# A spectral token mixer and FP8 MLP: one layout of quarter tiles for the whole spectrum

## The chip, the cores and the metric

The kernel runs on one core of a Trainium2 chip. The metric is the device time of one execution in microseconds (us), the median of several runs. One launch computes the whole layer, all weights and tables included, from HBM to HBM in float32 with the quantised MLP in between.

## The reference

The input x is (8, 128, 128, 96): batch, height, width, channel. The layer is

```python
x = x + conv(layernorm_c(x))          # a global filter in the Fourier domain
t = x as tokens
x = t + ffn(layernorm_t(t))           # an MLP in float8 with float16 accumulation

# conv
x_pre = soa1_scale * relu(x @ w1.T)**2 + soa1_bias        # 96 -> 192 channels
xf    = rfft2(x_pre, over h and w)                         # 128 x 65 complex, 192 channels
filt  = cubic resize of three small complex filters to 128 x 65
r     = softmax over the 3 filters of an MLP of mean(x) and mean(relu(bn(x @ sp_w.T)))
xsp   = irfft2(xf * sum_s r[s] * filt[s])
y     = xsp @ w2.T                                         # 192 -> 96 channels

# ffn, q8 = rounding to float8e5, q16 = rounding to float16
h = relu(q16(q16(q8(x) @ q8(W1).T) + q8(b1)))              # 96 -> 384
y = q16(q16(q8(h) @ q8(W2).T) + q8(b2))
```

## The kernel before

Each of the 8 batches passes through three streams.

*Stream a* (`before`) works by units of four image columns w, 32 units a batch. x is read twice: as `xb` in blocks of 16 columns with h on the partitions, for the layer norm's statistics (`measure`, and on GpSimd, ACT and DVE the reciprocal root r), and as `xT`, half-blocks of 8 columns with the channel on the partitions. r goes through HBM (`store_r`, L650) and comes back copied to 96 partitions (`load_r`, L654). `scale` (L659, DVE) multiplies four columns of xT by r into one of three `zT` tiles; both inputs are read with a step of 8 elements, since w is the innermost index of xT and rB. `project` (L672, TensorE) multiplies by w1 and sp_w, ACT applies relu and the square, `transform` (L701) takes the real Fourier transform along h, and the result goes to HBM as Y, one row of (w, 192 channels) for each of the 128 row frequencies.

*Stream s* (`spectrum`) works by groups g of four such rows, 31 full ones and two special ones (frequencies 32 and 96, 0 and 64), 33 a batch. `load_y` (L842) brings four rows with w on the partitions, in runs of 768 bytes. `along_w` (L874) is a matmul along w with the channel on the output partitions. 192 channels are more than 128 partitions, so for the two rows of a pair the first 128 channels make a full tile each, and the remaining 64 of both share a third; `pack` (L866, GpSimd) copies those side by side into `yb`. `filters_of` (L887) makes the filters with 64-column tiles, DVE (L913, L916) multiplies, GpSimd (L923, L938, L940) adds and turns back to a real basis, giving `xf`. For every two groups (16 pairs a batch), the channels are mixed with w2 into two PSUM banks `pv`, one for each row of the pair: `mix_low` first clears the banks with matmuls of zeros (L971) and adds the shared tile in quarters of the 128x128 array (64 rows by 64 columns, L984); `mix` (L995) adds the two full tiles. Two copies on ACT (L1006, L1018) and a matmul (L1011) follow, and V goes to HBM.

*Stream c* (`after`) works by units of four columns in blocks of 16. `load_v` (L1117, L1118) reads x into `xr` and V into `vin`; `last` (L1123) finishes the inverse transform, `residual` (L1131) adds xr into `t`, then layer norm, rounding to float8, and the MLP: `first` (L1170), `accumulated` (L1177, ACT, to float16), `biased` (L1181, DVE: bias and maximum with 0 for each of three tiles of 128 hidden channels), `hidden` (L1185, ACT, to float8), `second` (L1192), then L1203, L1207, L1210 and the store (L1213).

The streams of different batches overlap: a of one batch runs beside s of the batch before and c of the one before that. The order of the instructions on each engine is fixed when the kernel is built. Every step is entered by `at(time, ...)` with a due time (the stream's start plus the unit's number times its period plus an offset from the table `O` or `OWN`) and the steps it comes after; `in_order` takes the steps by due time as their predecessors and PSUM banks allow, and the engines then follow that order. Loads and small stores are issued from SyncE, the stores of Y and V from ACT.

Of the kernel before, what the change touches and what calls it, by code (L numbers as in the profile page):

```python
# [56 lines left out]
NG = 31  # L57
# [210 lines left out]
def _columns(p, r):  # L268

    if p < NP - 1:  # L270
        return [(g, cs) for g in (2 * p, 2 * p + 1) for cs in range(2)]
    return [(NG - 1, 0), (NG - 1, 1)] + [(NG, 0), (NG, 1)] * (r == 0) + [(NG + 1, 0)]
# [98 lines left out]
def metaformer_kernel(ctx: ExitStack, tc: tile.TileContext, a: dict, out: bass.AP):  # L371
    nc = tc.nc
    x, xT = a["x"], a["xT"]
# [49 lines left out]
    zeros = const.tile([128, 64], mybir.dt.bfloat16, name="zeros")  # L423

    NZT = 3
    zTs = [const.tile([C + 1, QW, 128], F32, name=f"zT{i}") for i in range(NZT)]
# [8 lines left out]
    w2A = load(T_CONST, "w2A", [128, C], a["w2T"][:128, :])  # L435
    w2B = const.tile([128, C], F32, name="w2B")
# [4 lines left out]
    b1q = const.tile([128, NHC], F32, name="b1q")  # L441
# [3 lines left out]
    def projection(sp):  # L445
# [36 lines left out]
        def others():  # L482
            for i in range(2):
                nc.sync.dma_start(out=w2B[64 * i : 64 * i + 64, :], in_=a["w2T"][128:, :])
            make_identity(nc, ident)
            nc.vector.tensor_copy(ident8, ident, saturate=False)
            nc.vector.memset(ones, 1.0 / (H * W))
            nc.vector.memset(zeros, 0.0)

            nc.vector.tensor_scalar(soa_bias, soa_bias, 128.0, None, ALU.mult)  # L490
# [6 lines left out]
    def filters(sp):  # L497
# [38 lines left out]
        def weights():  # L536
# [15 lines left out]
            nc.vector.tensor_copy(b1q, b1h)  # L552
# [69 lines left out]
    def before(b, t0, P):  # L622
# [4 lines left out]
        one = named("a", b, {None: NU, **dict.fromkeys(blocks, NWB), "load_xT": NU // 2, "load_r": NU // 2})  # L627
# [4 lines left out]
        def load_x(blk):  # L632
            if blk == 0:
                kept["gacc"] = pa.tile([C, NU], F32, name="gacc", tag="gacc")
            xb = pa.tile([128, WB, C], F32, name="xb", tag="xb")
            nc.sync.dma_start(out=xb, in_=x[b, :, blk * WB : (blk + 1) * WB, :])
            kept["x", blk] = xb
# [6 lines left out]
        def load_xT(hb):  # L644
            t = kept["xT", hb] = pa.tile([C, H, HB], F32, name="xT", tag="xT")
            nc.sync.dma_start(out=t, in_=xT[b, hb, :, :, :])

        def store_r(blk):
            t = kept["Rd", blk] = dram.tile([2, H, HB], F32, name="Rd", tag="Rd")
            nc.sync.dma_start(out=t.rearrange("f h w -> h f w"), in_=kept["r", blk].rearrange("h (f w) -> h f w", f=2))  # L650

        def load_r(hb):
            t = kept["rB", hb] = pa.tile([C, H, HB], F32, name="rB", tag="rB")
            nc.sync.dma_start(out=t, in_=kept["Rd", hb // 2][hb % 2].partition_broadcast(C))  # L654

        def scale(u):
            hb, q = divmod(u, 2)
            w = slice(q * QW, (q + 1) * QW)
            nc.vector.scalar_tensor_tensor(  # L659
                zTs[(b * NU + u) % NZT][:C, :, :],  # L660
                kept["xT", hb][:, :, w].rearrange("c h w -> c w h"),
                1.0,
                kept["rB", hb][:, :, w].rearrange("c h w -> c w h"),
                ALU.mult,
                ALU.mult,
                accum_out=kept["gacc"][:, u : u + 1],
            )

        def project(u, i0):
            px = kept["px", u, i0] = bank("px")[:, : 2 * (MED + SCTX)]  # L670
            for i in range(2):
                nc.tensor.matmul(  # L672
                    px[:, i * (MED + SCTX) : (i + 1) * (MED + SCTX)],
                    lhsT=zTs[(b * NU + u) % NZT][:, i0 + i, :],
# [42 lines left out]
        for u in range(NU):  # L717
            t = t0 + u * P
            blk, q = divmod(u, NQ)
            if q == 0:  # L720
# [3 lines left out]
                at(t + o["a_store_r"] * P, store_r, blk, after=[one("rest", blk)])  # L724
            if q % 2 == 0:
                hb = u // 2
                after = [one("scale", u - 4 + n) for n in (0, 1)]
                at(t + o["a_load_xT"] * P - 3, load_xT, hb, after=after)
                at(t + o["a_load_r"] * P, load_r, hb, after=after + [one("store_r", blk)])
            at(t + o["a_measure"] * P, measure, blk, q, after=[one("load_x", blk), one("rest", blk - 2)])  # L730
            after = [one("load_xT", u // 2), one("load_r", u // 2)] + both("project", u - NZT)
            at(t + o["a_scale"] * P, scale, u, after=after)
            for i0 in (0, 2):
                after = [one("scale", u), one("square", u - 2), one("context", u - 2)]
# [88 lines left out]
        after = [one("context", NU - 1), one("scale", NU - 1)]  # L823
# [5 lines left out]
    def spectrum(b, t0, P):  # L829
# [9 lines left out]
        def load_y(g):  # L839
            assert stored[b] == NU  # L840
            yt = kept["yt", g] = psp.tile([128, 4, MED], F32, name="yt", tag="yt", bufs=3)
            nc.sync.dma_start(out=yt, in_=Y[b][4 * g : 4 * g + 4, :, :].rearrange("j w m -> w j m"))  # L842
# [16 lines left out]
        def pack(g):  # L859

            yb = kept["yb", g] = psp.tile([128, 2, 2, 64], F32, name="yb", tag="yb")
            yt = kept["yt", min(g, NG)]
            src = yt[:, :, 128:].rearrange("w (s k) m -> w s k m", s=2)
            if g == NG:
                src = yt[:, 0:2, 128:].unsqueeze(2).to_broadcast([128, 2, 2, 64])
            nc.gpsimd.tensor_copy(yb, src)  # L866

        def along_w(g, cs):
            yt, yb = kept["yt", min(g, NG)], kept["yb", g]
            ja, jb = (2 * cs, 2 * cs + 1) if g < NG else (cs, cs) if g == NG else (2, 3)  # L870
            both = yb[:, 1 if g > NG else cs, :, :].rearrange("w k m -> w (k m)")
            pz = kept["pz", g, cs] = bank("pz")
            for u, y in enumerate((yt[:, ja, :128], yt[:, jb, :128], both)):
                nc.tensor.matmul(  # L874
                    pz[:, u * 2 * L : (u + 1) * 2 * L], lhsT=y, rhs=F2[:, cs, :], start=True, stop=True
                )

        def filters_of(g):
# [3 lines left out]
            halves = [(u, h, u * MED + 64 * h) for u in range(2) for h in range(2)]  # L882
            halves += [(2, k, k * MED + 128) for k in range(2)]
            for u, h, m0 in halves:
                for s in range(2 if g <= NG else 1):
                    p = slice(64 * s, 64 * s + R)
                    nc.tensor.matmul(  # L887
                        pf[64 * h : 64 * h + 64, s, u * 2 * L : (u + 1) * 2 * L],
                        lhsT=tb[p, m0 : m0 + 64],
                        rhs=RW[p, :],  # L890
                        start=True,
                        stop=True,
                    )
# [53 lines left out]
        def alone_t(g):  # L947
            z = kept["dm", g]
            nc.vector.tensor_tensor(z[:, 0, 0, 0:1], z[:, 0, 0, 0:1], soa_bias, ALU.add)
            nc.vector.tensor_tensor(z[:64, 2, 0, 0:1], z[:64, 2, 0, 0:1], soa_bias[:64], ALU.add)  # L950
# [12 lines left out]
        def mix_low(p):  # L963

            for r in range(2):
                kept["pv", p, r] = bank("pv")
            for h in range(2):
                for r in range(2):
                    half, rows = slice(64 * h, 64 * h + 64), slice(64 * r, 64 * r + 64)
                    n = len(_columns(p, r)) * C  # L970
                    nc.tensor.matmul(  # L971
                        kept["pv", p, r][half, :n],
                        lhsT=zeros[rows, :64],
                        rhs=zeros[rows, :1].to_broadcast([64, n]),
                        start=True,
                        stop=False,
                    )
            for i in range(5):
                for h in range(2):
                    for r in range(2):  # L980
                        if i < len(_columns(p, r)):
# [4 lines left out]
                                lhsT=kept["xf", g][rows, cs, 2, half],  # L986
                                rhs=w2B[rows, :],
                                start=False,
                                stop=False,
                            )  # L990

        def mix(p):
            for r in range(2):
                for i, (g, cs) in enumerate(_columns(p, r)):
                    nc.tensor.matmul(  # L995
                        kept["pv", p, r][:, i * C : (i + 1) * C],
                        lhsT=kept["xf", g][:, cs, r, :],
                        rhs=w2A,
                        start=False,
                        stop=(i == len(_columns(p, r)) - 1),  # L1000
                    )

        def mixed(p, r):
            n = len(_columns(p, r)) * C
            v = kept["V", p, r] = psp.tile([128, 5 * C], F32, name="V", tag="V")
            nc.scalar.copy(v[:, :n], kept.pop(("pv", p, r))[:, :n])  # L1006

        def invert(p, r):
            n = len(_columns(p, r)) * C
            pg = kept["pg", p, r] = bank("pg")  # L1010
            nc.tensor.matmul(pg[:, :n], lhsT=GL, rhs=kept.pop(("V", p, r))[:, :n], start=True, stop=True)  # L1011

        def inverted(p, r):
            if r == 0:
                kept["gst", p] = psp.tile([128, 8 * C], F32, name="gst", tag="gst")
            n = len(_columns(p, r)) * C
            lo = 0 if r == 0 else 8 * C - n
            nc.scalar.copy(kept["gst", p][:, lo : lo + n], kept.pop(("pg", p, r))[:, :n])  # L1018
# [10 lines left out]
        filled = [op.key for op in ops if b == 0 and op.key[1] in ("row_put", "padding", "others", "w2A", "GL", "SEL")]  # L1029
# [8 lines left out]
        for g in range(NG + 2):  # L1038
            t = t0 + g * P
            pz0, pz1 = one("along_w", g, 0), one("along_w", g, 1)  # L1040
            ty = min(g, NG)
# [293 lines left out]
```

## Time and profile before

| | |
|---|---|
| median of 3 runs | 2752.21 us (2751.84 to 2757.75) |
| span of the profiled execution | 2754.4 us |
| busy: DVE, ACT, POOL | 2276.1, 2233.0, 2122.2 us |
| moved by DMA | 618.05 MB in 480,023 packets |
| yt from Yd | 256 transfers of 384 KB |
| xT from in_xT | 128 transfers of 384 KB |

Busy times are of the whole execution and of all three streams; since these overlap, an engine's share says nothing yet of what waits for what. An entry of a group of instructions gives the line, the engine, what is written from what, the shape of one, the count, then the busy time in us and the mean of one in ns, and after the second bar how long the engine stood idle just before them. A float32 matmul stands as two instructions.

### The profile page before, as it was taken

Reading aid. Unit: us, or ns where it says so; the run is one execution under the profiler, and the core shown is the slowest. Engines: PE = TensorE matmul, PEld = TensorE weight load, DVE = VectorE, ACT = ScalarE, POOL = GpSimd, SP = SyncE. Lnnn points to the kernel's source line nnn. Section 1 sums busy time; section 2 is a strip of 40 time slices with the busy share of each in tenths; the row PEclk is TensorE's granted clock in tenths of the full one; section 3 lists DMA queues with packets and bytes.
Section 4 is the critical chain, followed back from the end, with each engine's and each line's share of the span. In section 5 each row is a group of like instructions: output and inputs, shape, how many; then the busy total and the mean of one; then the engine's idle time right before and its main releaser. Section 6 shows DMA issues by size and latency. Waiting matters only on the chain.

```text
span 2754.4 us, 69406 instructions
## 1 busy us (share of the span) xinstructions
PE 2567.8 (93%) x25130; PEld 1953.0 (71%) x25130; DVE 2276.1 (83%) x5887; ACT 2233.0 (81%) x4452; POOL 2122.2 (77%) x3246
## 2 busy tenths in 40 slices
PE   4989999999999999999999999999999998999765
PEld 2668877777677777777677777777777776677433
DVE  3557667798898999889898889889889878999786
ACT  2665556699888879889998878889988997888898
POOL 1239997888788878988688969888788886889432
PEclk9899999999999999999999999999999998999896
DMA  7888777977688866878687757888777774656441
GB/s 205 263 263 253 242 224 241 287 233 251 209 255 260 252 213 196 271 242 262 220 258 245 243 171 220 273 259 257 231 239 242 230 222 147 185 178 190 149 129 62
DMA packets 480023, 618.05 MB, mean 224 GB/s; under 512 B 174542, under 2 KB 381270, under 8 KB 479658
## 3 DMA queue, kind: packets, MB, share of 16 engines
q1 hardware_dynamic: 424386, 462.60, 56.8%
q10 hardware_dynamic: 55296, 151.02, 14.7%
q8 instruction: 199, 3.26, 0.5%
q14 instruction: 142, 1.16, 0.1%
HBM read 405.36 MB, written 208.16 MB: 223 GB/s over the span
## 4 chain that ended last, share of the span: by engine, by line
PE 68%; DVE 13%; ACT 7%; POOL 4%; DMA 4%; issue 3%; SPq 1%; POOLq 0%; ACTq 0%; DVEq 0%
PE px L672 13%; PE pz L874 10%; PE py L701 10%; PE pv L995 7%; PE pf L887 6%; PE pg L1011 5%; PE ph L1170 4%; PE pk L1123 4%; PE po L1192 3%; PE pv L984 3%; DVE t L916 3%; DVE y L1181 2%; ACT h L1185 2%; ACT y L1177 2%; DVE st L581 2%
## 5 line engine op out<-in xcount | busy, mean ns | idle before, releaser
L923 POOL TENSOR_TENSOR rr<-t,t 128x390 f32<-128x390 f32 x512 | 520.4, 1017 | 60.4 <-DVE t L916 60.0
L672 PE MATMUL px<-W1S,zT 97*128 97x240 f32 x2048 | 519.4, 379 | 34.1 <-DVE zT L659 29.2
L1177 ACT CAST y<-ph 128x512 f16<-128x512 f32 x768 | 456.0, 603 | 24.2 <-PE ph L1170 22.4
L672 PEld LDWEIGHTS px<-W1S,zT 97*128 97x128 f32 x2048 | 377.2, 194 | 130.0 <-issue 33.7
L1151 ACT ACTIVATE z<-t,ln_m,ln_r 128x96 fp8e5<-128x96 f32 x960 | 461.2, 492 | 8.6 <-POOL ln_m L614 5.7
L1181 DVE TENSOR_SCALAR y<-y,b1q 128x512 f16<-128x512 f16 x768 | 427.5, 568 | 28.2 <-ACT y L1177 25.6
L683 ACT ACTIVATE rl<-px 128x480 f32<-128x480 f32 x512 | 295.7, 581 | 177.5 <-PE px L672 160.2
L701 PE MATMUL py<-X,F 128*128 128x384 f32 x1024 | 430.7, 507 | 2.1 <-ACT X L690 1.9
L1185 ACT ACTIVATE h<-y 128x1536 fp8e5<-128x1536 f16 x256 | 386.2, 1509 | 2.2 <-DVE y L1181 1.6
L659 DVE SCALAR_TENSOR_TENSOR zT<-xT,rB 96x512 f32<-96x512 f32 x256 | 339.8, 1328 | 53.1 <-DMA rB<-Rd 26.5
L874 PEld LDWEIGHTS pz<-F,yt 128*128 128x128 f32 x2080 | 301.4, 192 | 72.0 <-DVE t L1131 5.9
L1210 POOL TENSOR_TENSOR t<-t,o 128x1536 f32<-128x1536 f32 x64 | 210.1, 3282 | 167.8 <-DVE o L1207 165.8
L874 PE MATMUL pz<-F,yt 128*128 128x130 f32 x2080 | 329.0, 281 | 10.2 <-DVE t L1131 4.7
L857 POOL TENSOR_TENSOR tb<-tb,r 128x384 f32<-128x384 f32 (+1 forms) x264 | 287.0, 1087 | 59.7 <-DVE r L808 23.1
L916 DVE TENSOR_TENSOR t<-dm,pf 128x390 f32<-128x390 f32 x512 | 282.6, 552 | 43.8 <-PE pf L887 18.4
L1170 PE MATMUL ph<-zT,W1q 96*128 96x512 fp8e5 x768 | 293.5, 397 | 19.1 <-DVE zT L1166 13.9
L708 ACT COPY yst<-py 128x384 f32<-128x384 f32 x512 | 246.4, 486 | 74.3 <-PE py L701 67.8
L916 DVE TENSOR_TENSOR t<-dp,pf 128x390 f32<-128x390 f32 x512 | 280.3, 548 | 0.0
L940 POOL TENSOR_TENSOR xf<-rr 128x378 f32<-128x378 f32 x256 | 255.3, 997 | 19.7
L995 PEld LDWEIGHTS pv<-w2A,xf 128*128 128x128 f32 x2048 | 246.8, 194 | 13.6 <-issue 1.5
L995 PE MATMUL pv<-w2A,xf 128*128 128x96 f32 x2048 | 255.2, 278 | 0.0
L938 POOL TENSOR_TENSOR xf<-rr 128x390 f32<-128x390 f32 x256 | 250.1, 977 | 0.0
(126 smaller groups left out, 5210.5 us busy)
## 6 DMA issues: line engine op xcount, KB each, us to landing
Yd<-yst ACTq DMA_DIRECT2D x256, 384.0 KB
yt<-Yd SPq DMA_DIRECT2D x256, 384.0 KB
xb<-in_x SPq DMA_DIRECT2D x64, 768.0 KB
xT<-in_xT SPq DMA_DIRECT2D x128, 384.0 KB
rB<-Rd SPq DMA_DIRECT2D x128, 384.0 KB
tb<-T SPq DMA_DIRECT2D x256, 192.0 KB
Vd<-gst ACTq DMA_DIRECT2D x128, 384.0 KB
xr<-in_x SPq DMA_DIRECT2D x64, 768.0 KB
```

Source lines behind the costliest of these rows:

```text
L659: nc.vector.scalar_tensor_tensor(zTs[(b * NU + u) % NZT][:C, :, :], kept["xT", hb][:, :, w].rearrange("c h w -> c w h"), 1.0, kept["rB", h ...
L672: nc.tensor.matmul(px[:, i * (MED + SCTX) : (i + 1) * (MED + SCTX)], lhsT=zTs[(b * NU + u) % NZT][:, i0 + i, :], rhs=W1S, start=True, stop ...
L701: nc.tensor.matmul(py, lhsT=F1, rhs=kept["X", u][:, i0 : i0 + 2, :].rearrange("h w m -> h (w m)"), start=True, stop=True)
L874: nc.tensor.matmul(pz[:, u * 2 * L : (u + 1) * 2 * L], lhsT=y, rhs=F2[:, cs, :], start=True, stop=True)
L916: nc.vector.tensor_tensor(work(name, g), kept[d, g], pair(g, sign, c), ALU.mult)
L923: nc.gpsimd.tensor_tensor(kept["rr", g][:, :, 2 * i : 2 * i + 2, :], kept[ta, g], kept[tb, g][:, :, ::-1, :], op)
L995: nc.tensor.matmul(kept["pv", p, r][:, i * C : (i + 1) * C], lhsT=kept["xf", g][:, cs, r, :], rhs=w2A, start=False, stop=(i == len(_column ...
L1151: nc.scalar.activation(z, t, AF.Identity, bias=m, scale=r, saturate=False)
L1170: nc.tensor.matmul(kept["ph", u, n], lhsT=W1q[:, n * 128 : (n + 1) * 128], rhs=kept["zT", u], start=True, stop=True)
L1177: nc.scalar.copy(kept["y", u][:, n, :], kept.pop(("ph", u, n)))
L1181: nc.vector.tensor_scalar(y, y, b1q[:, n : n + 1], 0.0, ALU.add, ALU.max)
L1185: nc.scalar.activation(kept["h8", u], kept["y", u], AF.Copy, saturate=False)
```

## The change

The whole spectrum takes the layout that only the last 64 channels had. The 192 channels are three parts q of 64; a tile has the two rows of a pair on its two halves of 64 partitions, and q is an index beside them. So all three parts are treated alike, the copy in `pack` is not needed, and all mixing is done in quarters of the array. The rows are brought side by side by the loads themselves: one transfer for each row, in runs of 256 bytes. In the mixing the first matmul of each bank and half sets the start flag, in place of the zeros.

```diff
 def load_y(g):
-    yt = psp.tile([128, 4, MED], ...)
-    nc.sync.dma_start(out=yt, in_=Y[b][4 * g : 4 * g + 4, :, :].rearrange("j w m -> w j m"))
+    yt = psp.tile([128, 2, 3, 2, 64], ...)
+    for cs in range(2 if g <= NG else 1):
+        j = 4 * g + 2 * cs if g < NG else 4 * NG + cs if g == NG else 4 * NG + 2
+        for k in range(2):
+            row = j + (k if g != NG else 0)
+            nc.sync.dma_start(out=yt[:, cs, :, k, :], in_=Y[b][row, :, :].rearrange("w (q m) -> w q m", q=3))
-def pack(g):
...
-def mix_low(p): ...
-def mix(p): ...
+def mix_part(p, columns):
+    for i in columns:
+        for q in range(3):
+            for h in range(2):
+                for r in range(2):
+                    g, cs = _columns(p, r)[i]
+                    half, rows = slice(64 * h, 64 * h + 64), slice(64 * r, 64 * r + 64)
+                    nc.tensor.matmul(
+                        kept["pv", p, r][half, i * C : (i + 1) * C],
+                        lhsT=kept["xf", g][rows, cs, q, half],
+                        rhs=w2C[rows, q, :],
+                        start=(i == 0 and q == 0),
+                        stop=(i == 3 and q == 2),
+                    )
+mix_low: mix_part(p, (0, 1))
+mix:     mix_part(p, (2, 3))
```

The last pair's banks now have four columns each; before they had five and three.

In stream a, xT and r are laid out with h innermost, xT is loaded straight into one of four zT tiles, and one operation scales eight columns in place, without steps. xb comes from a copy of x in which each block is contiguous, with (w, h // 16) on the partitions.

```diff
-zTs = [const.tile([C + 1, QW, 128], ...) for i in range(3)]
+zTs = [const.tile([C + 1, HB, 128], ...) for i in range(4)]
-def scale(u):      # 512 elements, 32 a batch
-    scalar_tensor_tensor(zTs[..][:C], xT[:, :, w].rearrange("c h w -> c w h"), 1.0, rB[:, :, w].rearrange("c h w -> c w h"), ...)
+def scale(hb):     # 1024 elements, 16 a batch
+    scalar_tensor_tensor(z, z, 1.0, rB, ALU.mult, ALU.mult, accum_out=gacc[:, hb : hb + 1])
...
-after = [one("scale", u - 4 + n) for n in (0, 1)]
+after = both("project", u - 2 * NZT) + both("project", u - 2 * NZT + 1)
 at(t + o["a_load_xT"] * P - 3, load_xT, hb, after=after)
```

In stream c, the bias is kept spread over a tile of float16, one addition covers all three tiles of hidden channels, and the maximum is taken in the cast that follows. x is loaded straight into t, which has five buffers in place of four, and the residual is added in place.

```diff
-def biased(u, n):
-    y = kept["y", u][:, n, :]
-    nc.vector.tensor_scalar(y, y, b1q[:, n : n + 1], 0.0, ALU.add, ALU.max)
+def biased(u):
+    y = kept["y", u]
+    nc.vector.tensor_tensor(y, y, b1q, ALU.add)
 def hidden(u):
-    nc.scalar.activation(kept["h8", u], kept["y", u], AF.Copy, saturate=False)
+    nc.scalar.activation(kept["h8", u], kept["y", u], AF.Relu, saturate=False)
```

The due times in `STREAMS`, `O` and `OWN` are the same in both kernels.

## The prediction

> **What bounds the kernel now.** I read the page's shares first, then the busy time by stretch, then the groups kept apart by shape, then the DMA queues and SyncE's own waits.
>
> ```profile
> PE 2567.8 (93%) x25130; PEld 1953.0 (71%) x25130; DVE 2276.1 (83%) x5887; ACT 2233.0 (81%) x4452; POOL 2122.2 (77%) x3246
> ...
> PEclk9899999999999999999999999999999998999896
> DMA  7888777977688866878687757888777774656441
> ```
> ```profile
> 200.00:456.00 256.00, 254.32 (x2626) 202.95 (x2624) 183.36 (x452) 149.00 (x283) 229.73 (x316) 0.99 0.76 238
> ...
> 1200.00:1500.00 300.00, 294.02 (x2872) 222.77 (x2872) 267.00 (x712) 278.11 (x568) 248.90 (x386) 0.99 0.79 246
> ...
> 2540.00:2754.00 214.00, 141.43 (x1133) 87.33 (x1131) 159.27 (x458) 186.52 (x345) 77.70 (x148) 0.82 0.35 110
> ```
>
> In the second view the columns after the length are PE, PEld, DVE, ACT, POOL, the granted clock, the DMA share and GB/s. From 200 to 2540 us TensorE is busy 98% of the time (2277 of 2340 us over the ten windows of that answer), at full clock: there TensorE's own stream is the time. ACT comes next (278 of 300 us at its fullest). Before 200 us DMA is the limit (share 0.81 to 0.90 from 40 to 200 us); after 2540 us ACT is (187 of 214 us). So TensorE time saved in the middle 2340 us counts in full; time saved on DVE or POOL counts only where TensorE waits for them, and all TensorE idle in the middle is 63 us.
>
> ```profile
> L995 PE MATMUL pv<-w2A,xf 128*128 128x96 f32 x2048 | 255.2, 278 | 0.0
> ...
> L984 PE MATMUL pv<-w2B,xf 64*64 64x96 f32 x4096 | 112.9, 246 | 0.0
> L971 PE MATMUL pv<-zeros 64*64 64x384 bf16 x480 | 45.2, 348 | 2.3 <-DVE t L1131 1.1 <-DVE dp L913 0.7 <-DVE dm L913 0.2
> ```
> ```profile
> 1399.88 0.36 PE L971 MATMUL pv<-zeros 64*64 64x384 bf16 x4
> ...
> 1400.07 0.83 PE L984 MATMUL pv<-w2B,xf 64*64 64x96 f32 x32
> ...
> 1400.83 0.68 PE L1192 MATMUL po<-W2q,h 128*128 128x96 fp8e5 x12
> ...
> 1401.35 1.99 PE L995 MATMUL pv<-w2A,xf 128*128 128x96 f32 x16
> ...
> 1403.18 0.84 PE L701 MATMUL py<-X,F 128*128 128x384 f32 x2
> ```
>
> Those are the mixing groups over the run, and one pair of row groups in the timeline (start, length). A matmul's printed length overlaps the next one, so I use starts: zeros 0.19 us, 32 quarter instructions 0.76 us, 16 full ones 1.83 us. Each fp32 matmul is two instructions.
>
> ```profile
> L1181 DVE TENSOR_SCALAR y<-y,b1q 128x512 f16<-128x512 f16 x768 | 427.5, 568 | 28.2 <-ACT y L1177 25.6
> L659 DVE SCALAR_TENSOR_TENSOR zT<-xT,rB 96x512 f32<-96x512 f32 x256 | 339.8, 1328 | 53.1 <-DMA rB<-Rd 26.5 <-DMA xT<-in_xT 10.1 <-PE py L701 6.3
> ...
> L1207 DVE TENSOR_TENSOR o<-o,b2q 128x1536 f16<-128x1536 f16 x64 | 67.4, 1054 | 16.1 <-ACT o L1203 15.3
> ```
> ```profile
> L866 POOL COPY yb<-yt 128x256 f32<-128x256 f32 x264 | 138.5, 525 | 9.8 <-DMA yt<-Yd 9.8
> ```
> ```profile
> q1 hardware_dynamic: 424386, 462.60, 56.8%
> q10 hardware_dynamic: 55296, 151.02, 14.7%
> ```
> ```profile
> SPq L842 <- PE pz L874: 514.5, 151, 10.7
> ```
>
> These are the DVE and POOL groups that the change touches, the two DMA queues (71.5% of the 16 engines' span) and SyncE's longest wait: it is held up by buffers of yt, not by its own issue time.
>
> [...]four quarters take 4 x 0.76/32 = 0.095 us, one full instruction 1.83/16 = 0.114 us for the same multiplications. Across the trace's matmul records, the start before a quarter run comes about 0.09 us later than before other work (0.31 against 0.22 us after L1170), and the start after it about 0.09 us later than streaming alone gives (0.19 against 0.08 to 0.11). [...]The trace's packet records have no 256-byte packets, but 15 ns for 192 bytes, 25 for 384, 41.5 for 768 and 131 for 3072, so no cliff shows.
>
> **Part by part.**
>
> 1. *Mixing in quarters.* Removed per pair: 4 zero matmuls and 16 full instructions; 32 quarter instructions become 96. By starts: before 0.19+0.76+1.83 = 2.78 us. After: 96 x 0.095/4 = 2.28 us, in two runs instead of one, so one more mode change, 0.09+0.09 = 0.18 us. Saving 2.78-2.28-0.18 = 0.32 us by this one pair. Averages over all pairs are more favourable, as most zero runs are slower: within runs, quarters start 20.4 ns apart and the last lasts 80 ns, so 96 of them in two runs take 2.08 us, while zeros (0.20), 32 quarters (0.71) and full ones (1.83) take 2.74; with mode changes, 0.16 before and 2 x 0.18 after, 2.90 becomes 2.44 us, a saving of 0.46. Taking the busy times of the groups, 255.2+112.9+52.3 = 420.4 us (the three shapes of zeros are 52.3) becomes 3 x 112.9 = 338.7: 82 us, or 0.64 us a pair, before the mode change; 0.46 after. I take 0.455 x 128 pairs = **58 us**, ends 41 and 82. All of it is on TensorE's stream in the middle.
>
> 2. *Scaling without strides.* 256 operations of 512 elements become 128 of 1024. The strided one costs 1.07 us without GpSimd beside it. [...]DVE: 340+20 (its accumulator reads) becomes 128 x (1.5+0.08) = 202, saving 158 us (ends 190 and 110). It lies beside TensorE's work. xT now lands in the four rotating zT tiles and waits for the projection of half-blocks four back: two half-blocks more of lead.
>
> 3. *One bias addition.* 768 x 568 ns become 256 additions of 1536 fp16 elements, the form of L1207 at 1.05 us: 270 us, saving 158 (ends 183 at the 957 ns median and 30 at 1.55 us). The maximum moves into ACT's cast, at no cost: still one activation over the same elements. hidden is now behind one 1.05 us operation rather than a third of it, some 0.5 us later a unit; it has half a unit's period (4 us) in the order to hide in.
>
> 4. *No pack.* POOL loses 264 copies, 138 us; along_w waits for the loads directly. GpSimd holds up TensorE little, so I count nothing here.
>
> 5. *Paired loads.* Per batch 32 loads of four rows become 31x4+4+2 = 130 loads. Packets: 131,072 of 768 bytes become 399,360 of 256. Between 192 and 384 bytes I estimate 18 ns: 399,360 x 18 - 131,072 x 41.5 = 1.75 ms over 16 engines, 109 us each, plus 784 x 16 semaphore packets of 10 ns, 8 us. DMA goes from 72% to (1992+117)/2682 = 79%, and the fullest middle window from 0.83 to about 0.89; the head runs at 0.86 to 0.90. So it stays hidden, nearly. SyncE issues 784 more DMAs of about 0.36 us, 282 us, out of its waits. Queued behind the four issues of a yt are tb, xT and rB, each up to 1.1 us later; the three yt buffers give three groups' time. I charge 6 us in all.
>
> 6. *The rest:* x in a contiguous layout, 64-byte runs for r, xr loaded into t (five buffers): same bytes, nothing.
>
> **Sum.** -58 (mixing), -12 (a fifth of the middle's 63 us of TensorE idle, as DVE falls from 2276 to about 1960 us[...]), -3 in the head (xT earlier; DMA still the limit), -3 in the tail (DVE 1.7 us shorter a block of 17.5, but ACT sets it), +6 (loads). 2752-70 = **2682 us**.
>
> **Rivals.**
> - *The loads become the bound.* If a 256-byte packet costs what one of 768 does, 268,288 more at 41.5 ns are 696 us an engine: 1992+696+8 = 2696 us of DMA, and at a share of 0.95 the kernel takes 2840 us. For it: the middle has windows of 0.83 already. Against: the records of 192 and 384 bytes. The mild form, an order that now holds up the queues, gives some 2765.
> - *The gain is used up by waits.* ACT gives nothing up and is at 93% in one stretch; mode changes cost more, or projections wait for the longer scaling. Half of the mixing is left, nothing else: 2752-25 = 2727 us.
> - *DVE counts for more.* The chain of waits gives DVE 13% of the span, 358 us; 14% less DVE time would take 50 us off it, with the 82 us of the groups' busy time: 2620 us. Against: TensorE's idle in the middle is 63 us in all.
>
> **How the numbers follow.** Near the forecast (2650 to 2710) 0.58; used up by waits 0.20, of which 0.03 within 0.2%; DVE counts for more 0.14; loads or order make it slower 0.08. Faster 0.89, same 0.03, slower 0.08. The range, 2635 to 2728, takes in the bounds of the mixing and the rival at 2727, and leaves out the slower cases, a little above it, and the deepest of the DVE case.
>
> **What would show it.** Right: quarter matmuls 12,288 at about 340 us busy and no full ones; TensorE still 97% or more in the middle; scaling at 1.2 to 1.5 us; the addition near 1.05 us; DVE under 2000 us; about 750,000 packets, DMA below 0.9 in every middle window. Wrong: DMA at 0.95 with TensorE waiting for pz or zT; quarter instructions more than 25 ns apart; ACT full in the middle; or TensorE idle well above 63 us.

## The result and the profile after

The changed kernel takes 2777.81 us (median of 4 runs, 2770.25 to 2788.19) against 2753.01 us for the kernel before, measured beside it: a ratio of 1.0085, with a 95% interval from 1.0059 to 1.0112. It is slower by some 23 us, where 2682 us were forecast. The profiled execution is the slowest of the four.

The chain of waits of the kernel before, then the page of the changed kernel, with its shares, granted clock and DMA, its larger DMA queue and its chain. The chain follows the work that ended last back to the start and gives each engine its share of it.

```profile
PE 68%; DVE 13%; ACT 7%; POOL 4%; DMA 4%; issue 3%; SPq 1%; POOLq 0%; ACTq 0%; DVEq 0%
```

```profile
PE 2545.2 (91%) x30762; PEld 1887.8 (68%) x30762; DVE 2035.8 (73%) x5110; ACT 2210.3 (79%) x4452; POOL 2063.5 (74%) x2983
...
PEclk9899999999999999999999999999999998999886
DMA  7888888978689867887788858888788775665431
...
q1 hardware_dynamic: 697138, 464.28, 60.7%
...
PE 60%; ACT 10%; POOL 9%; DMA 9%; DVE 6%; issue 5%; SPq 1%; ACTq 0%; POOLq 0%; DVEq 0%
```

Every engine is busy for less time than before, and yet the span is longer. The chain has moved: TensorE's share is 60% against 68%, GpSimd's 9% against 4%, DMA's 9% against 4%. DVE's share, at 13% the largest after TensorE before, is 6%. The busy time by stretch of the changed kernel (columns as in the prediction):

```profile
200.00:456.00 256.00, 248.87 (x3319) 195.28 (x3322) 160.96 (x420) 146.79 (x285) 202.11 (x285) 0.97 0.84 241
...
1200.00:1500.00 300.00, 287.64 (x3375) 214.95 (x3374) 234.04 (x603) 270.30 (x555) 243.53 (x350) 0.98 0.82 242
```

In the first stretch TensorE stood idle for 1.7 us before and for 7.1 us now; in the second, for 6.0 and 12.4. Over the same ten windows from 200 to 2540 us, idle rose from 63 to 106 us. The groups of the changed kernel, and before the last three those of GpSimd in the kernel before:

```profile
L958 PE MATMUL pv<-w2C,xf 64*64 64x96 f32 x12288 | 315.8, 251 | 7.3 <-ACT yst L702 2.8 <-DVE dp L901 1.6 <-issue 1.5
```
```profile
L1139 DVE TENSOR_TENSOR y<-y,b1q 128x1536 f16<-128x1536 f16 x256 | 288.2, 1126 | 56.1 <-ACT y L1135 55.5
...
L653 DVE SCALAR_TENSOR_TENSOR zT<-zT,rB 96x1024 f32<-96x1024 f32 x128 | 185.7, 1451 | 60.5 <-DMA rB<-Rd 46.0 <-DMA zT<-in_xT 14.5
```
```profile
L923 POOL TENSOR_TENSOR rr<-t,t 128x390 f32<-128x390 f32 x512 | 520.4, 1017 | 60.4 <-DVE t L916 60.0
L857 POOL TENSOR_TENSOR tb<-tb,r 128x384 f32<-128x384 f32 x256 | 278.9, 1089 | 59.7 <-DVE r L808 23.1 <-PE py L701 14.0 <-PE ph L1170 12.1
...
L938 POOL TENSOR_TENSOR xf<-rr 128x390 f32<-128x390 f32 x256 | 250.1, 977 | 0.0
```
```profile
L911 POOL TENSOR_TENSOR rr<-t,t 128x390 f32<-128x390 f32 x512 | 536.7, 1058 | 58.5 <-DVE t L904 57.5 <-DVE gc L747 0.6
L857 POOL TENSOR_TENSOR tb<-tb,r 128x384 f32<-128x384 f32 x256 | 286.5, 1119 | 122.8 <-DMA tb<-T 65.2 <-DVE r L804 27.7 <-PE pz L863 11.9
...
L926 POOL TENSOR_TENSOR xf<-rr 128x390 f32<-128x390 f32 x256 | 260.0, 1016 | 0.0
```

The sizes of the changed operations came out near the estimates: quarter matmuls 316 us busy (340 forecast), the addition 1.13 us (1.05), the scaling 1.45 (1.5). What the prediction had not priced is in the last group. GpSimd's operations without the pack are the same as before, but four of its five largest groups take longer (L911 1058 ns against 1017, L926 1016 against 977), and tb, whose load held GpSimd up for 5 us in the kernel before, holds it up for 67 in all:

```profile
POOL tb L857 <- DMA tb<-T: 5.3, 3, 2.7
```
```profile
POOL tb L857 <- DMA tb<-T: 66.7, 37, 5.9
```

These are the kernel before and the changed one: the wait in us, how often, and the longest.

### The profile page after: what moved, and what is told of

Its sections match the earlier page's. It is cut to its first block, busy times and chain, and to the rows that moved or that the text cites. A ratio compares the mean times of both kernels' runs of the same rounds, so it can differ in the third digit from the quotient of the medians.

```text
span 2786.4 us, 80592 instructions
## 1 busy us (share of the span) xinstructions
PE 2545.2 (91%) x30762; PEld 1887.8 (68%) x30762; DVE 2035.8 (73%) x5110; ACT 2210.3 (79%) x4452; POOL 2063.5 (74%) x2983
## 4 chain that ended last, share of the span: by engine, by line
PE 60%; ACT 10%; POOL 9%; DMA 9%; DVE 6%; issue 5%; SPq 1%; ACTq 0%; POOLq 0%; DVEq 0%
PE px L666 12%; PE pz L863 9%; PE py L695 9%; PE pv L958 8%; PE pf L874 5%; PE pg L980 4%; PE ph L1128 3%; PE pk L1085 3%; PE po L1150 3%; ACT y L1135 3%; POOL t L1168 2%; ACT h L1143 2%; DMA tb<-T 2%; ACT z L1109 2%; POOL rr L911 2%
## 5 line engine op out<-in xcount | busy, mean ns | idle before, releaser
L911 POOL TENSOR_TENSOR rr<-t,t 128x390 f32<-128x390 f32 x512 | 536.7, 1058 | 58.5 <-DVE t L904 57.5
L863 PEld LDWEIGHTS pz<-F,yt 128*128 128x128 f32 x3120 | 417.0, 194 | 82.3 <-DVE t L1091 9.0
L863 PE MATMUL pz<-F,yt 128*128 128x130 f32 x3120 | 443.0, 282 | 13.2 <-DVE t L1091 6.0
L695 PE MATMUL py<-X,F 128*128 128x384 f32 x1024 | 432.1, 509 | 8.6 <-ACT yst L702 3.9
L857 POOL TENSOR_TENSOR tb<-tb,r 128x384 f32<-128x384 f32 (+1 forms) x264 | 296.7, 1124 | 124.3 <-DMA tb<-T 66.7
L1139 DVE TENSOR_TENSOR y<-y,b1q 128x1536 f16<-128x1536 f16 x256 | 288.2, 1126 | 56.1 <-ACT y L1135 55.5
L958 PEld LDWEIGHTS pv<-w2C,xf 64*64 64x64 f32 x12288 | 274.2, 136 | 77.0 <-issue 32.9
L958 PE MATMUL pv<-w2C,xf 64*64 64x96 f32 x12288 | 315.8, 251 | 7.3 <-ACT yst L702 2.8
L1128 PE MATMUL ph<-zT,W1q 96*128 96x512 fp8e5 x768 | 297.4, 401 | 22.2 <-DVE zT L1124 8.8
L928 POOL TENSOR_TENSOR xf<-rr 128x378 f32<-128x378 f32 x256 | 263.0, 1027 | 19.7
L926 POOL TENSOR_TENSOR xf<-rr 128x390 f32<-128x390 f32 x256 | 260.0, 1016 | 0.0
L874 PEld LDWEIGHTS pf<-RW,tb 52*64 52x64 f32 x6240 | 173.3, 133 | 109.9 <-issue 55.8
```

The costliest lines, as they stand in the source:

```text
L695: nc.tensor.matmul(py, lhsT=F1, rhs=kept["X", u][:, i0 : i0 + 2, :].rearrange("h w m -> h (w m)"), start=True, stop=True)
L857: nc.gpsimd.tensor_tensor(kept["tb", g][p, :], kept["tb", g][p, :], rates[b][p, :], ALU.mult)
L863: nc.tensor.matmul(pz[:, q * 2 * L : (q + 1) * 2 * L], lhsT=y, rhs=F2[:, cs, :], start=True, stop=True)
L874: nc.tensor.matmul(pf[64 * k : 64 * k + 64, s, q * 2 * L : (q + 1) * 2 * L], lhsT=tb[p, m0 : m0 + 64], rhs=RW[p, :], start=True, stop=True,)
L911: nc.gpsimd.tensor_tensor(kept["rr", g][:, :, 2 * i : 2 * i + 2, :], kept[ta, g], kept[tb, g][:, :, ::-1, :], op)
L958: nc.tensor.matmul(kept["pv", p, r][half, i * C : (i + 1) * C], lhsT=kept["xf", g][rows, cs, q, half], rhs=w2C[rows, q, :], start=(i == 0 ...
```

## The experiments

All ratios are to the kernel before, measured beside each kernel on the same chip. Each kernel has a short name (e1, e2 and so on). Two kernels are compared through those ratios; times from ratios take 2753 us for the kernel before.

**The loads: number of transfers and length of runs.** The first edit puts one transfer in place of four, the second keeps four and takes whole rows, the third keeps the short runs in one transfer.

```diff
 # e1_one_load
+j0 = 4 * min(g, NG)
+flat = yt.rearrange("w s q k m -> w (s q k m)").rearrange("w (j m) -> w j m", j=4)
+nc.sync.dma_start(out=flat, in_=Y[b][j0 : j0 + 4, :, :].rearrange("j w m -> w j m"))
 # e2_four_long, for each cs and k
+flat = ...  # as in e1
+nc.sync.dma_start(out=flat[:, 2 * cs + k, :], in_=Y[b][row, :, :])
 # e3_one_short, yt is [128, 3, 4, 64]; the two special groups keep a transfer for each row
+nc.sync.dma_start(out=yt, in_=Y[b][j0 : j0 + 4, :, :].rearrange("j w (q m) -> w q j m", q=3))
```

> The changed kernel, but each group of rows comes in one transfer of four whole rows in runs of 768 bytes, as before the change. The channels of a pair's two rows then lie in the tile in another order than the mixing takes them for, so the values differ; sizes, engines and counts of everything else are the same. Theory A (the loads cost the gain: their issues on SyncE or their short runs): 2690 to 2720 us, and GpSimd's wait for tb falls from 67 us to under 20. Rival B (the loads are innocent; the new order of the steps, the longer scaling or the longer bias addition cost it): 2760 to 2790 us.

Measured (e1): 2724.67 us, 0.9905 (0.9884 to 0.9925). GpSimd waits 23 us for tb.

> The changed kernel with its four transfers a group, each of one row, but in runs of 768 bytes (values displaced as in the run with one transfer). Theory A1 (four issues a group in SyncE's queue hold up tb, xT and rB): within 10 us of the changed kernel, 2768 to 2788. Theory A2 (the short runs take DMA time): within 10 us of the run with one transfer. Rival B: all three the same, about 2778.

Measured (e2): 2761.56 us, 1.0041 (1.0025 to 1.0058). It lies between the two that the expectations named, 37 us over one transfer and 12 us under the changed kernel, and nearer to theory A1.

> The changed kernel with one transfer for each of the 31 full groups, still in runs of 256 bytes, into a tile laid out as w, q, row, channel; all values are as in the reference. Theory A1: near the run with one transfer of long runs, plus at most 10 us for DMA time: 2695 to 2730. Theory A2: within 10 us of the changed kernel. Rival B: about 2778.

Measured (e3): 2733.88 us, 0.9931 (0.9909 to 0.9953).

So the four transfers cost 37 us with long runs (1.0041 against 0.9905) and 42 us with short ones (1.0085 against 0.9931); the short runs themselves cost 7 to 12 us. The intervals of the pairs with one and with four transfers are apart. Those of e1 and e3 overlap, and those of e2 and the changed kernel only just don't, so the cost of short runs is barely resolved. The loads account for some 50 us, and the rival that they were innocent falls. SyncE's issues, from the answers on the tile yt of the kernel before, of the changed kernel, and of the kernels with one long, four long and one short transfer (shortest, median and longest in ns):

```profile
L842 SPq DMA_DIRECT2D yt<-Yd x256: 359/376/7223, 184.1 to 2528.0; - x128
```
```profile
L842 SPq DMA_DIRECT2D yt<-Yd x1040: 517/619/6702, 187.7 to 2556.7; - x174
```
```profile
L840 SPq DMA_DIRECT2D yt<-Yd x264: 359/371/5961, 188.3 to 2490.8; - x132
```
```profile
L843 SPq DMA_DIRECT2D yt<-Yd x1040: 319/430/6049, 183.9 to 2527.6; - x174
```
```profile
L840 SPq DMA_DIRECT2D yt<-Yd x248: 585/586/8270, 192.1 to 2486.6; - x124
```

A row in short runs takes 619 ns to issue, not the 360 of the estimate, so four take 2.5 us and not 1.4. That isn't the main thing: in e2 an issue takes 430 ns, near the estimate, and four transfers cost 37 us all the same. The timeline of SyncE in the changed kernel shows what can stand behind them:

```profile
1424.38 7.08 SPq L842 DMA_DIRECT2D yt<-Yd  x4
1431.55 0.89 SPq L1171 DMA_DIRECT2D out<-t  x1
1432.54 0.38 SPq L848 DMA_DIRECT2D tb<-T  x1
```

Here tb is issued only after 8 us of yt and a store. Between the end of a tb issue and the start of the operation that uses it, the traces have a median of 11.3 us in the kernel before and 9.4 in the changed one; e1 has 11.0, e2 10.2, e3 10.4.

By which wait the four transfers cost time, no run shows by itself, but the traces narrow it down. It isn't DMA time: the larger DMA queue has a share of 56.7% in e2 and 56.8% in e1. GpSimd's wait for tb doesn't follow the times either: it is 44 us in e2 and 42 in e3, which is 30 us faster, and 58 in e12 below, the fastest of all. DVE's waits for rB and xT are shorter in e2 than in e1 (37 against 49 us). What sets the kernels with four transfers apart is ACT. Its longest waits of the kind, in the kernel before, in the changed one and in e2:

```profile
ACT yst L708 <- DMA Vd<-gst: 4.5, 1, 4.5
ACT z L1151 <- DMA yt<-Yd: 2.7, 1, 2.7
```
```profile
ACT z L1109 <- DMA zT<-in_xT: 11.7, 3, 5.8
```
```profile
ACT z L1110 <- DMA rB<-Rd: 9.7, 4, 4.1
...
ACT y L1136 <- DMA tb<-T: 8.7, 2, 5.7
```

These operations don't read zT, rB or tb. In the traces the transfers of SyncE and ACT tell their landing by the same eight semaphores, taken in turn (1571 transfers in the kernel before, 2354 in the changed one). ACT, about to issue a store of Y or V, waits for an earlier transfer with the same semaphore to land, and that is mostly one of SyncE's (for 316 of its 384 stores in the kernel before and 321 in the changed one); ACT's other work stands behind it. With four transfers for one the turn comes round sooner: a semaphore is used again after 13.8 us on average in the kernel before and after 9.3 in the changed one. The idle time of ACT that the traces put down to a landing is in all 57 us in e2, 68 in the changed kernel and 80 in e13 below, the three with four transfers, and 1 to 18 us in the other thirteen kernels (9 before). This path is read from the traces; no run takes it away alone.

With one long transfer all other parts of the change still gain only 26 us, of 76 expected. So the parts were tried alone, on the kernel before. Theory C says that the mixing gives its 50 to 60 us and another part gives 30 to 40 of them back; theory D, that the mixing gives less than worked out and the other parts nothing. The new bias and the new scaling each need more SBUF than the kernel before leaves (a pool of 68.25 KB a partition, with 65.7 KB left beside the bias and 66.8 beside the scaling), so each was tried together with x loaded into t, which makes the room.

**x loaded into t.**

```diff
-xr = kept["xr", blk] = pools["c"].tile(...)
+xr = kept["t", blk] = pools["c"].tile([128, WB, C], F32, name="t", tag="t", bufs=5)
```

> The kernel before with one part of the change: x loaded straight into t, with five buffers, and the residual added in place. Both theories: 2745 to 2755; over 2765 would make this the part that gives the time back.

Measured (e6): 2755.41 us, 0.9998 (0.9983 to 1.0012). Nothing, as expected.

**The spectrum alone.** All of the change in the spectrum, with one short load as in e3; then with one long load as in e1; then with all quarters of a pair in one run.

```diff
 # e9_one_quarter_run
 def mix_low(p):
...
-    mix_part(p, (0, 1))
 def mix(p):
-    mix_part(p, (2, 3))
+    mix_part(p, (0, 1, 2, 3))
```

> The kernel before with the change of the spectrum alone: the paired rows (one load for a full group, in runs of 256 bytes), no pack, all mixing in quarters. Theory C: 2690 to 2705 us. Theory D: 2725 to 2740, the time of the kernel with all parts and one load.

Measured (e7): 2724.41 us, 0.9885 (0.9856 to 0.9913), at the edge of what theory D named and well short of C.

> The kernel before with the change of the spectrum alone, one load for every group in runs of 768 bytes (channels and rows displaced in the tile, so the values differ). If short runs cost by their DMA time, 2708 to 2718 us, as they cost 9 us in the kernel with all parts; if they cost only through SyncE's issues, 2720 to 2728.

Measured (e8): 2714.71 us, 0.9861 (0.9834 to 0.9887). The interval overlaps that of e7, so the 7 us of the short runs aren't resolved here.

> The spectrum's change alone (one load in short runs), with all 48 quarter matmuls of a pair in one run, at the place of the second. If each further run of quarters costs two mode changes of 0.09 us, 128 pairs save 23 us: 2698 to 2706. Rival: the time is set by what waits for the copies and the order, 2720 to 2728.

Measured (e9): 2716.29 us, 0.9863 (0.9834 to 0.9891). The interval overlaps that of e7: a gain of 6 us isn't resolved, and 23 us (0.0084) are ruled out only just, since e7's interval less 0.0084 ends at 0.9829.

The spectrum's change gains 38 us with the old run length. TensorE is busy for 2516.8 us in e8 against 2567.8 before, 51 us less, and stands idle for 15 us more over the whole span: that much of the saving came back as waits. The single run of e9 saves another 20 us of busy time (2500.7 against 2520.5 in e7), near the 23 expected, and 13 of these came back.

**Scaling and bias, each with x in t.** The edits are those of the change itself.

> The kernel before with x loaded into t and the scaling of eight columns without steps. Theory C: 2765 to 2775 us if it is the scaling (one operation of 1.45 us that both units of a half-block wait for, and xT loads that wait for TensorE instead of DVE). If it is innocent: 2740 to 2757.

Measured (e5b): 2745.24 us, 0.9974 (0.9963 to 0.9984): a gain of 7 us. GpSimd is busy for 2041 us here against 2122 in e6.

> The kernel before with x loaded into t (which alone changed nothing, and makes the room) and the bias added in one operation. Theory C (part of what is missing is given back by the bias or the scaling): 2765 to 2775 us if it is the bias. If the bias is innocent: 2740 to 2757.

Measured (e4b): 2788.55 us, 1.0127 (1.0102 to 1.0152): a loss of 35 us, with 78 us *less* DVE work. GpSimd's part in it, first in e6, then in e4b, which differ in the bias alone:

```profile
PE 2558.8 (93%) x25130; PEld 1948.5 (71%) x25130; DVE 2274.5 (83%) x5887; ACT 2232.1 (81%) x4452; POOL 2122.1 (77%) x3246
...
PE 68%; DVE 11%; ACT 7%; POOL 6%; DMA 5%; issue 3%; SPq 1%; POOLq 0%; ACTq 0%; DVEq 0%
```
```profile
PE 2586.7 (93%) x25130; PEld 1961.3 (70%) x25130; DVE 2196.5 (79%) x5375; ACT 2228.7 (80%) x4452; POOL 2271.1 (81%) x3246
...
PE 53%; POOL 20%; ACT 9%; DVE 7%; issue 5%; DMA 5%; SPq 1%; POOLq 0%; ACTq 0%; DVEq 0%
```
```profile
L938 POOL TENSOR_TENSOR xf<-rr 128x390 f32<-128x390 f32 x256 | 247.5, 967 | 0.0
```
```profile
L938 POOL TENSOR_TENSOR xf<-rr 128x390 f32<-128x390 f32 x256 | 282.8, 1105 | 0.0
```

GpSimd executes the same 3246 instructions and is busy 149 us longer; its share of the chain goes from 6 to 20%. The instructions and their shapes are the same, so the longer busy time is taken for waiting inside the operations.

**What of the bias costs: form or place.** Three kernels, each on the kernel before.

```diff
 # e10_place: one step, after all three casts
+def biased(u):
+    for n in range(NHC):
+        y = kept["y", u][:, n, :]
+        nc.vector.tensor_scalar(y, y, b1q[:, n : n + 1], 0.0, ALU.add, ALU.max)
 # e11_form: three steps at the old places, x in t
+nc.vector.tensor_tensor(y, y, b1q[:, n, :], ALU.add)
 # e14_one_scalar: one step
+nc.vector.tensor_scalar(kept["y", u], kept["y", u], b1q[:, 0:1], 0.0, ALU.add, ALU.max)
```

> The kernel before, with its three operations for the bias of a unit issued as one step, at the place and after the waits of the single addition. Theory L (the single addition costs because it reads two tiles of SBUF for 1 us at a stretch[...]): 2745 to 2760 us, GpSimd busy near 2120. Theory P (it costs because all three parts now wait for the last cast and the cast to float8 waits for all): 2775 to 2790 us, GpSimd busy near 2120.

Measured (e10): 2770.31 us, 1.0056 (1.0027 to 1.0084), GpSimd busy 2124 us.

> The kernel before with x in t, the three operations at their old places but in the new form: additions of two fp16 tiles of 512 elements[...], the maximum in the cast. Theory L: slower than before, 2765 to 2790 us, GpSimd busy 2200 or more. Theory P: 2745 to 2757 us, GpSimd near 2120.

Measured (e11): 2778.22 us, 1.0100 (1.0077 to 1.0123), GpSimd busy 2233 us.

> The kernel before with one scalar operation over all 1536 elements at the place of the single addition, with the first tile's bias for all three tiles, so that it reads one tile of SBUF only. Theory L: if what counts is two inputs, 2730 to 2755 us; if any long hold counts, up to 2770, with GpSimd busy above 2150. Theory P: 2775 to 2790 us.

Measured (e14): 2745.07 us, 0.9975 (0.9965 to 0.9985), GpSimd busy 2175 us.

Neither theory holds alone. The form costs 28 us by itself and brings 111 us of GpSimd time with it; the place costs 15 us (7 to 23 by its interval) and brings none. The six runs of e10 spread: two took 2758 to 2759 us at a granted clock of 0.970, four 2769 to 2777 us at 0.961 to 0.968. The third kernel has the place of the second theory and a single input, and is faster than before. It has 183 us less DVE work too, so it shows that a merged operation need not lose, and doesn't separate the two causes further. Its operation takes a median of 620 ns, 256 times, and GpSimd is busy 52 us longer.

**The bias undone in the changed kernel, and the parts that gained put together.** e13 is the changed kernel with the three old operations; e12 has the spectrum as in e9, the scaling and x in t, and the old bias.

> The changed kernel with one part undone: the bias is again three operations of one SBUF tile each, with the maximum in them. If the single addition costs inside the changed kernel what it cost alone (35 us): 2738 to 2750 us, and GpSimd's mean for the operations of the spectrum falls by 30 ns or more. Rival (in the changed kernel DVE is free enough that it costs nothing): 2770 to 2785.

Measured (e13): 2760.87 us, 1.0015 (1.0002 to 1.0029). GpSimd's L926 falls from 1016 to 918 ns and L911 from 1058 to 999. The gain is 17 us by medians, 19 by ratios, half of what the addition cost alone. Why it is half isn't shown.

```profile
L911 POOL TENSOR_TENSOR rr<-t,t 128x390 f32<-128x390 f32 x512 | 507.1, 999 | 92.2 <-DVE t L904 89.1 <-PE py L695 2.1 <-PE pz L863 0.2
```

Its wait for tb is larger still (87 us), though the kernel is faster: once more that wait doesn't follow the time.

> The parts that helped, together: quarter mixing in one run a pair, no pack, one load a group in short runs, the scaling without steps, x in t; the bias as before. If the parts add (2716 for the spectrum so, 8 less for the scaling): 2703 to 2713 us. Rival: DMA, busier by the short runs, gives the 8 us back: 2714 to 2722.

Measured (e12): 2705.28 us, 0.9823 (0.9800 to 0.9847), 49 us faster than the kernel before and faster than the changed one. The parts add: 38 (e9) and 7 (e5b) are 45.

**Where TensorE's time went.** In the traces the granted clock is either 1.0 or 0.5. In the kernel before, the matmuls of L995 start 112 ns apart at 1.0 and 213 at 0.5 (medians), those of L672 202 and 400. Busy time thus holds the work at full clock and what half clock adds to it, for which half of the busy time in the stretches of 0.5 is taken. So divided, the profiled executions are, in us:

| | span | work at full clock | added by half clock | idle |
|---|---|---|---|---|
| kernel before | 2754 | 2501 | 67 | 187 |
| changed kernel | 2786 | 2457 | 88 | 241 |
| e8 (spectrum, one long load) | 2718 | 2451 | 66 | 202 |
| e1 (one long load) | 2724 | 2453 | 65 | 206 |
| e2 (four long loads) | 2760 | 2457 | 74 | 230 |
| e6 (x in t) | 2746 | 2502 | 57 | 187 |
| e4b (bias and x in t) | 2789 | 2503 | 84 | 203 |

The work depends on the mixing alone: 2498 to 2505 us in every kernel with the old one, 2451 to 2457 with quarters in two runs, 2429 to 2431 with one run (e9, e12). The rest is lost in two ways. In all sixteen traces, each stretch of 0.5 between 200 and 2540 us follows 6.8 us in which TensorE had stood idle for 1.27 us or more, where 0.2 to 0.3 us are the average. So a wait seems to cost a second time, by the clock after it: of the 43 us between e6 and e4b, 27 are half clock and 15 idle, and of the 21 us between the kernel before and e10, 17 and 6, with slightly less work. No run changed the clock alone, so that the waits cause the drops is read from their order in time.

## Why the prediction was wrong, point by point

The sizes it named as signs of being right came, apart from DVE's time (2036 us, under 2000 forecast) and TensorE's share of the middle (95%, 97% forecast). Of its signs of being wrong, "TensorE idle well above 63 us" came: 106 us.

1. *TensorE bounds the middle.* Right, and used wrongly. TensorE is busy 97% of the middle (2277 of 2340 us), not 98%, and not all of that at full clock: the ten windows have a granted clock from 0.94 to 1.00. And the prediction's rule that other engines' time counts only through TensorE's 63 us of idle doesn't bound losses: idle went to 106 us, and half clock took 22 us more over the span.
2. *Mixing in quarters, 58 us.* The quarters stream as forecast: at full clock they start 21 ns apart (20.4 estimated). What the prediction calls a mode change is there too: in the changed kernel a run of quarters starts 0.31 us after the last matmul of L1128, other work (L863, L695) 0.22. The size was 50 us of TensorE's work (e8), and it didn't count in full: 15 us of it came back as idle, and 38 us are left in time. This is a mis-sized term.
3. *Scaling, hidden beside TensorE.* Right; 7 us in time. The 1.5 us of one scaling was the author's estimate and not shown by the kernel before. It takes 1.45 us on average, and 1.22 in the 22 cases with no GpSimd operation beside it; the strided one takes 1.07 us in the 31 cases without one and 1.36 with one.
4. *One bias addition.* This is the first step that failed. DVE's saving came (428 to 288 us), and the maximum cost ACT nothing, as forecast (a median of 1502 ns a cast, 1497 before). But the prediction took the saving for relief and left GpSimd out. In the trace of the changed kernel GpSimd's L911 takes 1398 ns on average in the 91 cases that overlap one of the additions (by 674 ns on average) and 984 in the others, L926 1450 and 938. In the kernel before, L923 takes 1023 ns where it overlaps the old operation and 1012 elsewhere, L938 983 and 973. DVE pays as well: the addition takes 954 ns on average with no GpSimd operation beside it and 1163 with one, the old operation 344 and 615 (up to 3182). The old one is over in as little as 253 ns; the new one takes 957 (the median, as for L1207 in the kernel before), 256 times. GpSimd paid 149 us for it in e4b, and the time 35 us (17 to 19 in the changed kernel). That the number of SBUF inputs counts fits the runs: two at the old places (e11) brought 111 us of GpSimd time, one at the new place (e14) 52. What inside an operation holds GpSimd up isn't shown. The extra wait, "half a unit's period to hide in", wasn't hidden either: 15 us in e10.
5. *Paired loads, 6 us.* The second step that failed, and the larger. DMA's share was nearly right (packets of 256 bytes took 18.9 ns on average against the 18 estimated). By byte these packets took 1.3 times as long as those of 768 bytes in the same trace (43.9 ns). What was wrong is that 784 more issues come out of SyncE's waits and that the buffers cover what is queued behind them. The number of transfers cost 37 to 42 us, the short runs 7 to 12. The prediction looked for the delay at tb, xT and rB; of these waits only tb's grew clearly with the four transfers, and it doesn't follow the times. What follows them is ACT, whose waits for landings went from 9 to 68 us and which the prediction had left out. That this carries the whole cost isn't shown.
6. *No pack.* GpSimd lost 138 us of copies. What that gained isn't separated from the mixing.

The sum by the runs is -38 (spectrum, one long load), -7 (scaling), +19 (bias, inside the others), +37 (four transfers) and +12 (short runs), which is +23 us, as measured. It closes because the +19 is what is missing between the first two, 45 us, and the 26 of e1; e13 gives the same 19 by itself.

Of the rivals, the mild form of the first came nearest: an order that holds up the queues, at some 2765 us. Its main form was wrong, since DMA stayed at 0.87 or less in every middle window. The rival of used-up waits is right in kind, but its 2727 us is still a gain (half of 58 would have been 29, not 25), and the third, that DVE counts for more, goes against e5b and e4b, where 149 and 78 us less of DVE work brought 7 us gained and 35 lost.

## What to carry to other kernels

Price an added transfer by all that may wait for it to be issued or to land, in other engines' streams too, and not by whether its own queue has time to spare. Where one engine's operations take longer beside another's, an operation's cost includes what it adds to the other: here 256 additions with two SBUF inputs for 768 operations with one saved 78 us of DVE's time and added 149 to GpSimd's (e4b). And where the most loaded engine has others at 80 to 90% behind it, count a part of any saving as lost to them (here 15 of 50 us), and count a wait of TensorE for more than its length (here 15 us more of idle went with 27 more of half clock, e4b against e6).

## What the runs showed of the hardware that was not expected

The time to issue a transfer from SyncE depends on its shape: at the least 319 ns for one row of 128 x 768 bytes, 359 for four such rows, 517 for one row in runs of 256 bytes, 585 for four rows in such runs. A scaling over 512 elements with steps of 32 bytes had a median of 1072 ns before 190 us, where GpSimd is busy for a quarter of the time, and 1024 elements without steps one of 1222 in the changed kernel: by element, fixed costs included, the strided form took 1.75 times as long. Mixing all in 64x64 quarters, without the zeros, took 50 us less of TensorE's work than mixing mostly in full instructions (e8), and one run of quarters a pair instead of two another 20 us, or 0.16 us a pair. And between 200 and 2540 us the granted clock fell to 0.5, for 3.4 us or a multiple of it, only after 6.8 us with 1.27 us or more of idle TensorE, though not after every such stretch.
